# Splitting the first weight chunk into two column halves, and the last values product into two halves of 128 columns

## The chip, the core and the metric

The kernel runs on one core of a Trainium2 chip. The time is the device time of one execution in microseconds (us); for the kernel before it is the median of three runs. The profile is of one further execution. TensorE (PE) multiplies, VectorE (DVE), ScalarE (ACT) and GpSimd (POOL) do the rest, and SyncE (SP) issues most transfers. In a profile "PEld" is TensorE's loading of a stationary operand, and "SPq", "ACTq" and "POOLq" are what the engines' sequencers issue.

## What is computed

For x of shape 2 x 2048 x 512 in float32 (cut from the reference):

```python
xn = _layernorm(x, axis=-1)
# attention on xn: a second layer norm with gamma and beta, one head of width 512, causal
q, k, v = x_norm @ qkv[:, :KEY], x_norm @ qkv[:, KEY:2 * KEY], x_norm @ qkv[:, 2 * KEY:]
s = softmax(causal(q @ k.T / sqrt(KEY))) @ v @ o_proj + residual
# mixture of experts on xn: 8 experts, the best 2 of each token, silu between two layers
g = _silu(_L0_ffn_ref(xn, ...))
x = x + s * g
```

## The kernel before, in words

The 4096 rows are 32 tiles of 128 rows, in 8 blocks of four tiles. A first stage multiplies weights with one another, so that later only two products of the normalized rows are needed: `wqk` is the product of the query and key weights (`fold`, L221), `wvo` that of the value weights and `o_proj` (`fold_by_seven`, L247). It also normalizes the rows block by block, makes queries and values from them and stores them to DRAM. A second stage routes the tokens and computes the experts. A third computes attention and the output, tile by tile, in pairs. Everything is float32, and from L867 on each engine gets its instructions in the order of the Python text (`manual_schedule`).

**The opening.** Six small matmuls on zeros (`warm`, L872) run while nothing has arrived. `load_raw(c, pair)` (L214) issues chunk `c` (128 rows of 512 columns) of two weights, the first of the pair on SP's queue and the second on ScalarE's. For chunk 0 of the first weight there are two transfers already, columns 0 to 127 and 128 to 511. After chunk 1, `load(0)` (L169) brings the rows of block 0, tiles 0 and 2 on SP's queue, 1 and 3 on ScalarE's. Then come chunks 2 and 3 of the pair, and four chunks of the second pair. Ten transfers stand in ScalarE's queue ahead of its first computation, the square root of the first block's variances in `rstd_of` (L130), with the load of its function table.

In the built program each transfer of the two hardware queues, SP's and ScalarE's together, takes the next of eight completion semaphores. The issue of a transfer waits until the one that had this semaphore before, eight places earlier, has landed. The numbering goes through both queues about alternately.

`fold` multiplies chunk by chunk: for each of the four chunks there are four matmuls, one for each block `r` of 128 rows of the result, into four accumulators `banks`. A float32 matmul of the text is two instructions in the profile, each with its own weight load. The first matmul takes the first 128 columns of chunk 0 of one weight as stationary operand and all 512 columns of chunk 0 of the other as moving operand.

Meanwhile VectorE takes statistics of the rows (`norm_stats`, L304), waits for ScalarE's root, and makes z (`norm_rows`, L326); GpSimd splits z into halves (`zu`, L347), SP turns these by transposing transfers (`zuT`, L354) and stores them (`zu_d`, L357). VectorE also makes the sums that `fold_by_seven` needs (L239, L245). Of each block ScalarE makes the keys `kT` (L379) and issues their store to `kt_d` (L384) from its own queue, among its copies of TensorE's results (L549, L552, L555, L569).

**The end.** The last two tiles, `AHEAD` (L1709), are finished by `values_end(s)` (L1618) with s = 30. The values of the pair come from seven products instead of eight, in halves of 256 columns, `LO` and `HI`. Accumulators are `p57`, `p64` and `p03`, from a pool of three banks that are taken in turn (`bank`, L1589). The last product is the lower half of the second tile: `chain` (L1576) over six blocks of the combined weights, and `product` (L1527) over the four blocks left over, both into `p64[:, HI]`. Before it stand in VectorE's order the preparations that don't need it: `u3` is multiplied by the gate and added to the gate's tile. Then `emit_ahead` (L1727) takes the product from its accumulator, multiplies it by the row's divisor and the gate (`gated`, L1723), adds the prepared part (L1596) and issues the store on SP's queue (L1731):

```python
def emit_ahead(s, o, cols, attention=None):
    xt, _ = gates[s]
    gated(o[:, cols], o[:, cols] if attention is None else attention, s, cols)
    add(o[:, cols], o[:, cols], xt[:, cols])
    nc.sync.dma_start(out=ob[:, seq[s], cols], in_=o[:, cols])
```

Of the kernel before, what the change touches and what calls it, by code (L numbers as in the profile page):

```python
# [20 lines left out]
P = 128  # L21
# [5 lines left out]
def gated_attention_moe(  # L27
# [28 lines left out]
    nc = tc.nc  # L56
    B, S, D = x.shape
# [8 lines left out]
    NK = KEY // P  # L66
# [147 lines left out]
    def load_raw(c, pair):  # L214
        for i, queue in zip(pair, (nc.sync, nc.scalar)):

            cuts = (0, P, D) if c == 0 and i == 0 else (0, D)
            for at in (slice(*cut) for cut in zip(cuts, cuts[1:])):
                queue.dma_start(out=parts[i][:, c, at], in_=srcs[i][ts(c, P), at])

    def fold(dst, lhs, rhs, scale):  # L221
        pws = banks
        for c in range(NK):
            for r in range(ND):
                nc.tensor.matmul(
                    pws[r], lhsT=lhs[:, c, ts(r, P)], rhs=rhs[:, c, :],
                    start=(c == 0), stop=(c == NK - 1),
                )
        for r in range(ND):
            nc.scalar.mul(dst[:, r, :], pws[r], scale)  # L230

# [641 lines left out]
    for c in range(NK):  # L873
        load_raw(c, (0, 1))
        if c == 1:
            load(0)
    for c in range(NK):
        load_raw(c, (2, 3))
    load_small()
    load(1)  # L880
    fill_rows()
    norm(0)
    fold(wqk, parts[0], parts[1], 1.0 / math.sqrt(KEY))
    fold_sums = four(4), four(5)
    for k in ((0,), (1,), (2, 3)):
# [384 lines left out]
    def place(s):  # L1270
        b, t = divmod(seq[s], BT)
        return b, t, b - b % NBB
# [142 lines left out]
    for i in range(NM):  # L1415
# [21 lines left out]
        for _ in range(3):  # L1437
            if i >= paired.stop and early:
                f, b, c = early.pop(0)
# [83 lines left out]
    def place_keys(s):  # L1523

        return place(s)[1] + 1 + (place(s)[0] - place(s)[2]) * BT

    def product(dst, s, k0, k1, cols, start=True):  # L1527

        first = place(s)[2]
        for k in range(k0, k1):  # L1530
            nc.tensor.matmul(  # L1531
                dst, lhsT=turned[s][:, ts(k, P)], rhs=avs[first + k // BT][:, k % BT, cols],
                start=(start and k == k0), stop=(k == k1 - 1),
            )
# [5 lines left out]
    LO, HI = slice(0, D // 2), slice(D // 2, D)  # L1540
# [35 lines left out]
    def chain(dst, a, v, stop=True):  # L1576
        n = a.shape[1]
        for k in range(n):
            nc.tensor.matmul(  # L1579
                dst, lhsT=a[:, k], rhs=v(k), start=(k == 0), stop=(stop and k == n - 1)  # L1580
            )

    def vt(s, i):
        return lambda k: avts[place(s)[2] + k // 2][:, k % 2, i, :]

    def raw(s, half, cols):
        return lambda k: avs[place(s)[2] + k // 2][:, 2 * (k % 2) + half, cols]

    def bank(s, name):  # L1589
        return ps_b.tile([P, D], F32, name=f"{name}_{s}", tag="b")  # L1590

    def half_d(s, name):
        return cp.tile([P, D // 2], F32, name=f"{name}_{s}", tag=name)

    def add(out, a, b):
        nc.vector.tensor_tensor(out, a, b, ALU.add)  # L1596
# [21 lines left out]
    def values_end(s, meanwhile=()):  # L1618
        m, _, _, a22, _, s2, _, s4 = combos.pop(s)
        p1, o1, p57 = seven.pop(s)  # L1620
        u2, u3 = half_d(s, "u2"), half_d(s, "u3")
        o2 = op.tile([P, D], F32, name=f"o_{s + 1}", tag="o", bufs=4)
        k1, k2 = place_keys(s), place_keys(s + 1)
        p64, p03 = bank(s, "p64"), bank(s, "p03")
        chain(p64[:, LO], s2, vt(s, 1))
        add(u2, p64[:, LO], p1)
        add(u3, p57[:, HI], u2)
        add(o2[:, HI], p57[:, LO], u3)
        add(u2, p57[:, LO], u2)
        product(p03[:, LO], s + 1, 2 * m, k2, HI)  # L1630
        chain(p03[:, HI], s4, raw(s, 1, HI), stop=False)
        product(p03[:, HI], s, 2 * m, k1, HI, start=False)
        add(o1[:, HI], p03[:, HI], u2)
        if s in AHEAD:
            emit_ahead(s, o1, HI)
        add(o2[:, HI], p03[:, LO], o2[:, HI])
        if s in AHEAD:
            emit_ahead(s + 1, o2, HI)
        for f in meanwhile:
            f()  # L1640
        if s in AHEAD:

            gated(u3, u3, s + 1, LO)
            add(gates[s + 1][0][:, LO], u3, gates[s + 1][0][:, LO])
        chain(p64[:, HI], a22, vt(s, 3), stop=False)
        product(p64[:, HI], s + 1, 2 * m, k2, LO, start=False)
        if s in AHEAD:
            emit_ahead(s + 1, o2, LO, p64[:, HI])
        else:
            add(o2[:, LO], p64[:, HI], u3)  # L1650
        outs[s], outs[s + 1] = o1, o2

# [68 lines left out]
    def gated(out, a, s, cols):  # L1721

        nc.vector.scalar_tensor_tensor(  # L1723
            out, a, sums[s], gates[s][1][:, cols], ALU.mult, ALU.mult
# [7 lines that stand above are left out]
# [24 lines left out]
    for s in range(NT + OUT + 2):  # L1756
# [92 lines left out]
        elif s == 3:  # L1849
# [8 lines left out]
            for f, *args in joins:  # L1858
                f(*args)
            values_end(0, [lambda: query_sums(s + 1, nc.vector)])  # L1860
        elif s == NT:
            emit_ahead(s - 2, seven[s - 2][1], LO)
            values_next(s - 2)
        elif fast and s % 2 == 0:
            values_first(s - 2)

            if s != NT - 2:
                values_next(s - 2)
        elif fast and s == NT - 1:
            values_next(s - 3)  # L1870
            values_end(
                s - 3,
                [lambda: join_p(s)] * len(halves[s])
                + [lambda: combine_p(s - 1, (1, 3)), lambda: gate(s - 1)]
                + [lambda: combine_p(s - 1, (2, 4))],
            )
        elif fast:
            values_end(s - 3)
        elif 0 <= s - 2 < NT and not (s - 1 < NT and by_te(s - 1)):
            values(s - 2)  # L1880
# [56 lines left out]
```

## Time and profile before

| | us |
|---|---|
| median of three runs (lowest, highest) | 1010.59 (1010.33, 1010.79) |
| the profiled execution: its time, its span | 1012.02, 1010.3 |
| TensorE's first instruction | 1.13 |
| VectorE's first statistics | 8.40 |
| first 256-column pass of the last product | 1001.98 |
| transfer of the last store, issue to landing | 1.7 |
| VectorE, ScalarE, GpSimd: idle within the span | 29%, 60%, 52% |

The span goes from the first to the last instruction on the core, and the execution's own time has some 1.7 us more. The page gives the granted TensorE clock as full over the whole span. The core's transfers are busy to 80% and more in the first seven slices of 25 us, at 230 to 330 GB/s.

Views used below are the page itself, the timeline (instructions of an engine in order of time, like ones merged: start, duration, engine, line, operation, output<-input, shapes, count, and in brackets the idle time before it with what ended it), the list of waits, the groups by line and shape, and the transfers of a window. A wait is put down to the releaser that came last by the profile.

### The profile page before, as it was taken

To read this page: it belongs to the slowest core of one execution; us is meant where nothing else is said; L and a number is where in the kernel's file an instruction comes from. 1 tells how busy PE (TensorE), PEld (TensorE's weight loads), DVE (VectorE), ACT (ScalarE), POOL (GpSimd) and SP (SyncE) were. 2 spreads that over 40 slices of the span, in tenths; PEclk is the share of its full clock that TensorE was granted. 3 is DMA by queue.
4 is the path that set the end of the run, shared out by engine and by line. 5 is a ranking of instruction groups with operands and counts; after the bars stand their busy time and mean duration, and the time that the engine had idled before them with its cause. 6 is when DMAs were issued, how large, how long until landed. Compare 5 with 4: busy or idle time off the path is not lost. (4 is left out here: it accounts for less than half of the span.)

```text
span 1010.3 us, 13408 instructions
## 1 busy us (share of the span) xinstructions
PE 1001.5 (99%) x3924; PEld 665.7 (66%) x3924; DVE 719.6 (71%) x1396; ACT 402.7 (40%) x804; POOL 481.6 (48%) x475
## 2 busy tenths in 40 slices
PE   9999999999999999999999999999999999999998
PEld 5887888874577677667653448677675544447577
DVE  6997755896877777776744669678576457878667
ACT  3354455322444544444455122232345544442241
POOL 4474465003744444443432256164557776764272
PEclk9999999999999999999999999999999999999999
DMA  8799987979999999999999576373677768753361
GB/s 291 234 240 319 319 237 268 331 254 230 182 247 213 205 219 218 210 211 214 213 213 254 162 191 149 90 189 110 186 199 233 224 202 241 204 146 86 95 164 42
DMA packets 295495, 207.96 MB, mean 206 GB/s; under 512 B 230648, under 2 KB 243704, under 8 KB 294400
## 3 DMA queue, kind: packets, MB, share of 16 engines
q1 hardware_dynamic: 280128, 155.17, 62.1%
q0 software_dynamic: 10400, 34.63, 12.6%
q10 hardware_dynamic: 4896, 17.30, 4.6%
q8 instruction: 34, 0.56, 0.2%
q14 instruction: 37, 0.30, 0.1%
HBM read 92.35 MB, written 60.03 MB: 151 GB/s over the span
## 5 line engine op out<-in xcount | busy, mean ns | idle before, releaser
L1191 PE MATMUL py<-arena,ht 128*128 (+3 forms) x396 | 176.7, 593 | 0.0
L1303 PE MATMUL ps<-k,q 128*128 128x512 f32 (+3 forms) x416 | 143.0, 495 | 0.3 <-PEq L1451 0.3
L1491 POOL COPY pu<-pT 128x1024 uint16<-128x1024 uint16 (+2 forms) x74 | 81.8, 1137 | 119.1 <-ACT pT L1481 59.2
L1162 POOL COPY hu<-h 128x704 uint16<-128x704 uint16 x66 | 61.8, 954 | 155.8 <-issue 121.7
L1191 PEld LDWEIGHTS py<-arena,ht 128*128 128x128 f32 (+3 forms) x396 | 71.8, 185 | 80.6 <-issue 76.4
L1303 PEld LDWEIGHTS ps<-k,q 128*128 128x128 f32 x416 | 74.7, 190 | 67.1 <-issue 56.3
L966 POOL DMA_INDIRECT xs<-zu_d,toki x66 | 77.7, 1177 | 70.6 <-DVE toki L793 55.9
L1177 ACT ACTIVATE ht<-ht,b1sel 128x128 f32<-128x128 f32 (+3 forms) x216 | 67.9, 380 | 88.4 <-DVE ht L1171 88.4
L1141 DVE TENSOR_TENSOR h<-p,h 128x176 f32<-128x176 f32 x182 | 55.4, 336 | 59.6 <-PE p L1134 56.1
L1674 POOL DMA_INDIRECT yg<-y_d,posi x64 | 67.3, 1052 | 36.9 <-DVE yg L1685 22.0
L1531 PE MATMUL po<-v,pT 128*128 128x512 f32 x152 | 67.9, 592 | 0.0
L347 POOL COPY zu<-z 128x1024 uint16<-128x1024 uint16 x32 | 39.4, 1230 | 57.7 <-DVE z L332 57.7
L1481 ACT ACTIVATE pT<-pT,nm 128x1024 f32<-128x1024 f32 x14 | 16.1, 1148 | 110.3 <-DVE nm L1391 72.0
L1513 DVE COPY pT<-puT 128x1024 uint16<-128x1024 uint16 (+2 forms) x74 | 53.4, 750 | 7.4 <-DMA puT<-pu 7.2
L1199 ACT COPY y<-py 128x512 f32<-128x512 f32 x55 | 32.1, 584 | 62.1 <-PE py L1191 48.2
L1481 ACT ACTIVATE pT<-ps,nm 128x512 f32<-128x512 f32 (+3 forms) x52 | 30.0, 580 | 60.4 <-DVE nm L1391 36.7
L1361 DVE TENSOR_TENSOR pT<-p,pT 128x512 f32<-128x512 f32 x49 | 32.9, 687 | 25.8 <-PE p L1355 22.1
L1531 PEld LDWEIGHTS po<-v,pT 128*128 128x128 f32 x152 | 28.6, 190 | 31.9 <-issue 30.1
L1042 DVE COPY xT<-xhT 128x1024 uint16<-128x1024 uint16 x66 | 44.7, 703 | 6.4 <-DMA xhT<-xs 6.3
L1703 POOL TENSOR_TENSOR o<-o,yg 128x512 f32<-128x512 f32 x30 | 41.4, 1380 | 14.3 <-DVE o L1695 14.2
L1695 DVE SCALAR_TENSOR_TENSOR o<-xo,xscale,o 128x512 f32<-128x512 f32 x30 | 25.9, 871 | 30.1 <-ACT o L1692 30.1
L1704 POOL TENSOR_TENSOR o<-o,xo 128x512 f32<-128x512 f32 x30 | 43.2, 1439 | 2.4
(342 smaller groups left out, 2146.9 us busy)
## 6 DMA issues: line engine op xcount, KB each, us to landing
y_d<-y SPq DMA_DIRECT2D x66, 256.0 KB, 4.3
zu_d<-zu SPq DMA_DIRECT2D x32, 264.0 KB, 3.2
kt_d<-kT ACTq DMA_DIRECT2D x8, 1024.0 KB, 8.2
q<-qt_d SPq DMA_DIRECT2D x32, 256.0 KB, 5.0
k<-kt_d SPq DMA_DIRECT2D x32, 256.0 KB, 4.2
v<-v_d SPq DMA_DIRECT2D x32, 256.0 KB, 5.7
xo<-in_x_dram SPq DMA_DIRECT2D x32, 256.0 KB, 4.0
x<-in_x_dram SPq DMA_DIRECT2D x30, 256.0 KB, 6.5
```

The costliest lines, as they stand in the source:

```text
L966: nc.gpsimd.indirect_dma_start(out=xs, out_offset=None, in_=zu_d, in_offset=bass.IndirectOffsetOnAxis(ap=toki[:, order[i] : order[i] + 1], ...
L1042: nc.vector.tensor_copy(xT.bitcast(U16).rearrange("p c (t h) -> p c t h", h=2), xhs.pop(i).rearrange("p (h c) t -> p c t h", h=2),)
L1141: nc.vector.tensor_tensor(out, x, y, ALU.add)
L1162: nc.gpsimd.tensor_copy(hu[:, :, :H], h.bitcast(U16).rearrange("p (d h) -> p h d", h=2))
L1177: nc.scalar.activation(ht[:hn, c, at], ht[:hn, c, at], AF.Silu, bias=b1sel[:hn, c, j : j + 1])
L1191: nc.tensor.matmul(py[at, :], lhsT=ht[:k, c, at], rhs=rhs[n], start=(c == 0), stop=(c == NH - 1),)
L1303: nc.tensor.matmul(ps[:, :w], lhsT=aqs[seq[s] // 2][:, c, ts(t % 2, P)], rhs=aks[first + j][:, c, :w], start=(c == 0), stop=(c == ND - 1),)
L1481: nc.scalar.activation(turned[s][:, at:end], src, AF.Exp, bias=nm, accum_out=rs[:, j : j + 1])
L1491: nc.gpsimd.tensor_copy(pu[:, : 2 * w].rearrange("p (h d) -> p h d", h=2), turned[s][:, k : k + w].bitcast(U16).rearrange("p (d h) -> p h ...
L1513: nc.vector.tensor_copy(turned[s][:, k : k + w].bitcast(U16).rearrange("p (i t h) -> p i t h", t=P, h=2), puT[:, : 2 * w // P, :].rearrang ...
L1531: nc.tensor.matmul(dst, lhsT=turned[s][:, ts(k, P)], rhs=avs[first + k // BT][:, k % BT, cols], start=(start and k == k0), stop=(k == k1 - 1),
L1674: nc.gpsimd.indirect_dma_start(out=y, out_offset=None, in_=y_d, in_offset=bass.IndirectOffsetOnAxis(ap=posi[k][:, n : n + 1], axis=0),)
```

## The change

Chunk 0 of the second weight of the first pair, which was one transfer of 512 columns on ScalarE's queue, becomes two of 256 columns there. The first matmul of `fold` becomes two, one for each half of the columns, into the halves of the same accumulator; only the first of them starts the accumulation.

In `values_end`, for the last pair only, the last product is made in two halves of 128 columns one after the other, the first into its old place in `p64`, the second into the same columns of a further bank `p6` from the same pool. Each half is finished and stored by its own `emit_ahead`. All other pairs keep the old form.

```diff
     def load_raw(c, pair):
         for i, queue in zip(pair, (nc.sync, nc.scalar)):
 
-            cuts = (0, P, D) if c == 0 and i == 0 else (0, D)
+            cuts = (0, D) if c else {0: (0, P, D), 1: (0, D // 2, D)}.get(i, (0, D))
             for at in (slice(*cut) for cut in zip(cuts, cuts[1:])):
                 queue.dma_start(out=parts[i][:, c, at], in_=srcs[i][ts(c, P), at])
...
         for c in range(NK):
             for r in range(ND):
-                nc.tensor.matmul(
-                    pws[r], lhsT=lhs[:, c, ts(r, P)], rhs=rhs[:, c, :],
-                    start=(c == 0), stop=(c == NK - 1),
-                )
+                for h in (slice(0, D // 2), slice(D // 2, D)) if r + c == 0 else (slice(0, D),):
+                    nc.tensor.matmul(
+                        pws[r][:, h], lhsT=lhs[:, c, ts(r, P)], rhs=rhs[:, c, h],
+                        start=(c == 0 and h.start == 0), stop=(c == NK - 1), skip_group_check=True,
+                    )
...
-        chain(p64[:, HI], a22, vt(s, 3), stop=False)
-        product(p64[:, HI], s + 1, 2 * m, k2, LO, start=False)
         if s in AHEAD:
-            emit_ahead(s + 1, o2, LO, p64[:, HI])
+            for cols in (slice(0, P), slice(P, 2 * P)):
+                dst = (bank(s, "p6") if cols.start else p64)[:, HI][:, cols]
+                chain(dst, a22, lambda k: vt(s, 3)(k)[:, cols], stop=False)
+                product(dst, s + 1, 2 * m, k2, cols, start=False)
+                emit_ahead(s + 1, o2, cols, dst)
         else:
+            chain(p64[:, HI], a22, vt(s, 3), stop=False)
+            product(p64[:, HI], s + 1, 2 * m, k2, LO, start=False)
             add(o2[:, LO], p64[:, HI], u3)
```

## The prediction

> **What bounds the kernel now.** I read the engine shares first, then TensorE's waits, then the first 14 us and the last 10 us instruction by instruction.
>
> ```profile
> PE 1001.5 (99%) x3924; PEld 665.7 (66%) x3924; DVE 719.6 (71%) x1396; ACT 402.7 (40%) x804; POOL 481.6 (48%) x475
> ...
> PE bank_a L526 <- ACT raw L552: 1.4, 1, 1.4
> PE warm L872 <- DVE b1s L181: 1.1, 1, 1.1
> PE bank_b L526 <- ACT bank_c L555: 0.7, 1, 0.7
> ```
>
> TensorE is busy 1001.5 of 1010.3 us, so a change of its first and last microseconds can only move the 9 us that are left, unless it moves a wait inside. Those waits (each line: who waited for whom, total us, times, longest) are few. The longest, 1.4 us, decides what a gain at the start is worth.
>
> The opening (start, duration in us, then engine and what it did):
>
> ```profile
> 0.81 0.90 ACTq L219 DMA_DIRECT2D raw<-in_qkv_t_dram  x2
> 1.13 2.93 PE L872 MATMUL warm<-gw 128*128 128x128 f32 x12 [1.13 <-DVE b1s L181]
> 4.06 0.50 PEld L225 LDWEIGHTS bank_a<-raw 128*128 128x128 f32 x2 [0.30 <-DMA raw<-in_qkv_t_dram]
> 5.92 1.19 PE L225 MATMUL bank_b<-raw 128*128 128x512 f32 x2
> 7.50 4.06 ACTq L219 DMA_DIRECT2D raw<-in_o_proj_dram  x4
> 11.59 1.28 ACT L130 ACT_TABLE_LOAD   x1 [11.59 <-DMA raw<-in_qkv_t_dram]
> 12.88 0.21 ACT L130 ACTIVATE sd_a<-va 128x8 f32<-128x8 f32 x1
> 13.13 0.20 DVE L132 RECIPROCAL r_a<-sd_a 128x8 f32<-128x8 f32 x1 [0.94 <-ACT sd_a L130]
> ```
>
> Two things are to be seen. The first real weight load comes 0.30 us after the last one of the warming passes; it waits for data. And ScalarE's first computation waits until its own queue has issued ten transfers: the last issue ends at 11.56, the table load follows, then the root, and VectorE has stood 0.94 us for it. From 13.13 to 66 us the waits of VectorE show none on TensorE, and on ScalarE only its next root (0.27 us): its chain (fold sums, statistics, roots, rows for GpSimd, transposes) runs at its own pace from that root on.
>
> Where that chain meets TensorE:
>
> ```profile
> 81.49 0.33 ACTq L384 DMA_DIRECT2D kt_d<-kT  x1
> 82.34 0.59 ACT L552 COPY raw<-bank_a 128x512 f32<-128x512 f32 x1
> 82.99 1.99 PE L526 MATMUL bank_a<-kT,wqk 128*128 128x256 f32 x8 [1.40 <-ACT raw L552]
> ```
>
> ScalarE stands idle for 4.55 us before L569, because the store of block 2's keys ahead of it in its queue is not issued before 81.49. In the built program a transfer's issue waits for the one eight places earlier; here that is a store of `zu` of block 3 on SP, whose rows GpSimd had finished at 73.1 from z of VectorE's 65.6. So TensorE's 1.40 us come from VectorE's chain, not from its own past: what TensorE gains before 82.99 it waits there.
>
> **What the Trainium skill says.** "DMA: Bandwidth & Descriptors", section Queues, rings and completion order: each DMA engine goes round-robin between the queues, packet by packet. The trace agrees; from 3.0 to 3.2 us the two queues (ScalarE's q10, SP's q1; packets, MB, share) moved as many packets each, of unlike size:
>
> ```profile
> q10 hardware_dynamic: 29, 0.05, 64.4%
> q1 hardware_dynamic: 30, 0.03, 40.8%
> ```
>
> "TensorE: Matmul & The Clock Gate", What's actually happening: the array runs at half rate until it was busy for a window of about 3.4 us. Here passes of 512 columns start 0.85 apart (5.07, 5.92) and 0.43 apart from 6.5 on; so time won before the switch is worth half, unless the switch comes earlier too. The same page, section "Wait — 56ns, not 53.3ns?", gives a fixed cost of about 2.5 ns per matmul; halving columns therefore costs something, and the trace has the price itself (below).
>
> **Part 1, the first chunk.** The transfers are numbered about alternately on the two queues. By their issue waits, ScalarE's first (256 KB, chunk 0 of the keys' weights) landed at about 4.03, where SP's fifth issue starts, and SP's first (64 KB) by 3.78, where ScalarE's fifth starts. So the 256 KB are the gate, as halving them supposes. Eight packets per engine of SP's first and ScalarE's first are 4 + 16 = 20 KB; with the half they are 4 + 8 = 12 KB. 16 engines x 8 KB = 128 KB at the 0.39 MB/us of that stretch: 0.33 us sooner, 3.7. The warming passes start 0.227 apart, the last at 3.63, so the weight load can go at about 3.75 instead of 4.06: 0.3 us. The second half lands by the 16th packet, 32 KB, about 4.4, and is wanted 0.85 later than the first, at 4.7; SP's remaining 192 KB landed at 4.85, wanted at about 5.1 as before. Four passes of 256 take the place of two of 512 (0.2155 us apart against 0.43: nothing). Worth: 0.15 (switch of the clock stays) to 0.3 us.
>
> What is queued behind the added issue: ScalarE's eleven instead of ten transfers. Its queue gets packets one for one with SP's, so every later transfer of it lands eight packets per engine later. Before, its transfers land beside SP's in rounds of eight packets: at 20 KB per engine 4.0, at 48 KB 5.0, at 80 KB 7.3 (SP's third, by the issue at 7.1; ScalarE's third, 7.5), at 112 KB 8.5, at 144 KB 9.6 to 10.2, at 176 KB 11.1 to 11.2. The last is ScalarE's chunk 3, for which its last issue waits. After, chunk 3 is the seventh instead of the sixth transfer there, and lands with SP's seventh at 12 + 20 + 5 x 32 = 192 KB. SP's seventh landed at 12.0 with 208 KB, so 192 KB lie at 11.6. The last issue, table load, root and so VectorE's chain: 0.4 us later (bounds: 0, if the order of the numbers lets the issue wait on SP's earlier transfer or if va, ready at 12.19, were the gate; 0.65, a whole 256 KB). Nothing hides it: the next op of VectorE is the one that had waited 0.94. The inputs of the statistics land earlier or as before, so they hide nothing either. TensorE itself wants this chain's z at 18.5 (done 16.8, then 17.2) and s, t at 22.8 (18.4, then 18.8): covered. At 82.99 it isn't: TensorE restarts 0.4 us later and its early start is swallowed; I expect 1.4 + 0.4 + 0.2 = 2.0 us of wait there. Part 1: +0.4.
>
> **Part 2, the last product.**
>
> ```profile
> 777.68 1.06 PE L1303 MATMUL ps<-k,q 128*128 128x128 f32 x8
> ...
> 1001.98 2.75 PE L1579 MATMUL p<-vT,pT 128*128 128x256 f32 x12
> 1004.57 1.89 PE L1531 MATMUL p<-v,pT 128*128 128x256 f32 x8
> 1006.50 0.48 DVE L1723 SCALAR_TENSOR_TENSOR o<-p,ri,yg 128x256 f32<-128x256 f32 x1 [0.74 <-PE p L1531]
> 1007.02 0.42 DVE L1596 TENSOR_TENSOR o<-o,xo 128x256 f32<-128x256 f32 x1
> 1007.47 0.33 SPq L1731 DMA_DIRECT2D out_dram<-o  x1
> ```
>
> Now: 20 passes of 256 columns, (2.75 - 0.379)/11 = 0.2155 us apart, end 1006.46; then VectorE, SP, landing 1.7 us after the issue. After: 40 passes of 128. The row of 128 columns with own weight loads gives (1.06 - 0.275)/7 = 0.111 apart, so 39 x 0.111 + 0.275 = 4.60 from 1001.98: end 1006.58, +0.12 (bounds 0 and +0.25). The first half is done at 1001.98 + 19 x 0.111 + 0.275 = 1004.36; VectorE is at L1723 and L1596 for u3 until 1005.75, then does this half by 1006.45 and SP issues it by 1006.8: hidden. The second half: L1723 and L1596 lose 128 of 256 columns. L1308 (128x128) takes 0.292, L1596 at 256 columns 0.424, so 0.13 each, 0.27 in all. Store at 1006.58 + 0.04 + 0.39 + 0.29 + 0.03 = 1007.33 against 1007.47. Its packets: 1 KB ones took 46 ns each (1008.2 to 1008.8), 512-byte ones 28 ns (1.8 to 2.0); eight per engine: 0.37 against 0.23, -0.14 (0 to -0.2). Part 2: -0.14 - 0.14 = -0.28 (bounds -0.05 and -0.4). The second half's bank is the third request after the one of `p57`, whose last reader ended at 1000.44: no wait.
>
> **Sum.** +0.4 - 0.28 = +0.1 us. The profiled execution took 1012.02 for its span of 1010.3; the median of three runs is 1010.59, spread 0.46. I add the change to the median: 1010.7. What this kernel can tell from no change is about 0.2%, 2.0 us; both parts lie far below.
>
> **Rivals.**
> - VectorE's chain doesn't move: the last issue of ScalarE comes at 11.2 as before. For it: the two queues' numbers could be dealt so that the wait falls on SP's earlier chunk; against it: one transfer more in a queue that gets packets one for one. 1010.59 - 0.28 = 1010.3.
> - The start counts: the chain comes earlier, or the wait at 82.99 isn't its. For it: inputs land earlier; against it: root behind ScalarE's issues. 1010.59 - 0.28 - 0.3 = 1010.0.
> - Slower: the new bank isn't free. If the three banks turn so that the second half meets a tile whose reader is still to come (the first half's own), TensorE stops after 1004.36 until VectorE has read at 1006.12, and 4.60/2 us follow: store at about 1009.1, -0.14, so +1.5, with part 1 +1.9: 1012.5. It decides as soon as the second half's first pass starts after 1004.5. Against it: the count above.
>
> **Numbers.** Chain later (my forecast) 0.52, own range 1010.4 to 1011.1; chain unmoved 0.27; start counts 0.13; bank 0.04; something of the opening's shift growing on its way to 83 us (VectorE's ops there take 0.68 or 1.5 us beside GpSimd) 0.04. The range 1009.9 to 1011.3 leaves out the last two and a little of the third. Faster by over 0.2% would need 2 us from 9 us of idle: 0.03. Slower: half the bank's chance and of the last case: 0.04. Same: 0.93.
>
> **What would show it.** First weight load near 3.75; ACT table load near 12.0 and root near 13.3; wait for L552 near 2.0 us and bank_a starting near 83.4; last pass ending 1006.6 and last store issued 0.75 us after it, both moved by the shift. If the table load stays at 11.6, the second case holds; if bank_a starts before 82.9, the third. A sum over 2 us either way would mean a wait that I haven't seen.

## The result, and the profile after

| | median, us | runs (lowest, highest) | ratio to before, 95% interval |
|---|---|---|---|
| before | 1011.08 | 20 (1010.33, 1013.08) | |
| after | 1012.39 | 20 (1011.41, 1017.59) | 1.0014 [1.0008, 1.0021] |

The change costs 1.3 us, or 0.14%. The forecast was 1010.7, the range 1009.9 to 1011.3: the time lies above it. I had held about 0.2% to be the least that this kernel can tell from no change; with 20 runs of each, the interval of 0.14% lies clear of one. Of the 1.7 us between forecast and time 0.5 belong to the base, whose median over 20 runs is 1011.08 where three runs had given 1010.59. On that base the range would have ended at 1011.8, which is still too low.

The profiled execution after took 1012.14 us, span 1010.4. That of before took 1012.02, but it lay 0.9 above its median. So I profiled the kernel before a second time: 1010.95 us, span 1009.2. That execution, called the second profile below, is at the median; the one that the prediction used is the first.

The opening of the kernel after (timeline: start, duration, engine and instruction):

```profile
3.64 0.55 PEld L226 LDWEIGHTS bank_a<-raw 128*128 128x128 f32 x2
3.85 1.78 PE L226 MATMUL bank_a<-raw 128*128 128x256 f32 x4
...
8.15 0.30 PEld L226 LDWEIGHTS bank_a<-raw 128*128 128x128 f32 x2 [0.78 <-DMA raw<-in_qkv_t_dram]
...
11.99 0.30 PEld L226 LDWEIGHTS bank_a<-raw 128*128 128x128 f32 x2 [0.96 <-DMA raw<-in_qkv_t_dram]
...
13.67 1.28 ACT L130 ACT_TABLE_LOAD   x1 [13.67 <-DMA raw<-in_o_proj_dram]
14.97 0.21 ACT L130 ACTIVATE sd_a<-va 128x8 f32<-128x8 f32 x1
...
15.21 0.20 DVE L132 RECIPROCAL r_a<-sd_a 128x8 f32<-128x8 f32 x1 [2.35 <-ACT sd_a L130]
```

The start is 0.42 us earlier than before's 4.06, as meant. Then the transfers of chunks 1 and 2 come late, which the brackets of the third and fourth line show; and ScalarE's table load starts at 13.67 where it started at 11.59 (11.39 in the second profile). VectorE stands 2.35 us for the root instead of 0.94 (1.28 in the second profile).

The same 2 us can be followed to TensorE. First SP's transposing transfers and stores of block 3 in the kernel after, then the same lines of the kernel before in its second profile:

```profile
69.00 7.26 SPq L355 DMA_TRANSPOSE zuT<-zu  x4
76.31 2.98 SPq L358 DMA_DIRECT2D zu_d<-zu  x4
```

```profile
67.03 7.25 SPq L354 DMA_TRANSPOSE zuT<-zu  x4
74.33 3.41 SPq L357 DMA_DIRECT2D zu_d<-zu  x4
```

Then ScalarE and TensorE in the kernel after, at the place that the prediction had named, and TensorE there in the second profile of before:

```profile
81.99 0.33 ACTq L385 DMA_DIRECT2D kt_d<-kT  x1
82.36 0.58 ACT L570 COPY raw<-bank_c 128x512 f32<-128x512 f32 x1 [4.04 <-PE bank_b L527]
82.84 0.59 ACT L553 COPY raw<-bank_a 128x512 f32<-128x512 f32 x1
...
83.48 1.78 PE L527 MATMUL bank_a<-kT,wqk 128*128 128x256 f32 x7 [0.89 <-ACT raw L553]
```

```profile
81.92 1.99 PE L526 MATMUL bank_a<-kT,wqk 128*128 128x256 f32 x8 [0.84 <-ACT raw L552]
```

Put side by side (start of each step, us):

| step | before, first | before, second | after |
|---|---|---|---|
| table load | 11.59 | 11.39 | 13.67 |
| first reciprocal of VectorE | 13.13 | 12.93 | 15.21 |
| z of block 3 | 65.59 | 65.11 | 67.08 |
| block 3's transposing transfers (how long) | 67.51 (8.37) | 67.03 (7.25) | 69.00 (7.26) |
| block 3's stores of zu | 75.94 | 74.33 | 76.31 |
| store of block 2's keys | 81.49 | 80.42 | 81.99 |
| bank_a multiplied again | 82.99 | 81.92 | 83.48 |
| time of that execution | 1012.02 | 1010.95 | 1012.14 |
| time less the line above it | 929.03 | 929.03 | 928.66 |

Two things are to be seen. From the second profile to after the delay is 2.28 us at the root, 1.98 at the stores of zu, 1.56 where TensorE restarts. And what follows that restart takes the same time in every kernel of this document but one (no_cut, below): 928.9 to 929.1 us, with the new tail 928.7. So the moment at which TensorE gets on near 83 us sets the result. The first profile's extra 1.07 us arose on this chain as well: 0.20 at the root, 0.28 on VectorE up to the transposing transfers, 1.12 in those transfers themselves, and about 0.5 given back between the start of the stores of zu and the store of the keys.

TensorE's waits (total, times, longest) show the place as well, with one that is new, the third line:

```profile
PE bank_a L527 <- ACT raw L553: 0.9, 1, 0.9
PE bank_b L527 <- ACT bank_c L556: 0.7, 1, 0.7
PE bank_c L527 <- ACT raw L540: 0.7, 1, 0.7
```

The new wait lies at 49.7 us. Here are ScalarE and TensorE in the kernel after, then ScalarE in the second profile of before:

```profile
47.81 0.21 ACT L130 ACTIVATE sd_a<-va 128x8 f32<-128x8 f32 x1 [5.42 <-DVE va L319]
49.00 0.59 ACT L540 COPY raw<-bank_c 128x512 f32<-128x512 f32 x1
...
49.74 1.97 PE L527 MATMUL bank_c<-arena,wqk 128*128 128x256 f32 x8 [0.67 <-ACT raw L540]
```

```profile
45.84 0.21 ACT L130 ACTIVATE sd_a<-va 128x8 f32<-128x8 f32 x1 [4.05 <-DVE va L318]
47.03 0.59 ACT L539 COPY raw<-bank_c 128x512 f32<-128x512 f32 x1
```

ScalarE takes another block's root there as soon as VectorE's variances are ready, and that is 2.0 us later than in the second profile; its copies stand behind the root, and TensorE needs the last of them. So VectorE's late chain meets TensorE here already, before it does so near 83 us.

Why chunk 3 lands so late is in the transfers of the opening, from 3.5 to 6.5 us, first in the second profile of before and then after:

```profile
DMA packets 673, 1.19 MB, mean 396 GB/s; under 512 B 71, under 2 KB 162, under 8 KB 673
```

```profile
DMA packets 465, 0.78 MB, mean 259 GB/s; under 512 B 49, under 2 KB 130, under 8 KB 465
```

The issues agree: SP's seventh, which waits for a landing, comes at 7.94 after and at 6.29 in that profile.

The end of the kernel after:

```profile
1002.49 1.50 PE L1580 MATMUL p<-vT,pT 128*128 128x128 f32 x12
...
1006.06 1.06 PE L1532 MATMUL p<-v,pT 128*128 128x128 f32 x8
1006.18 0.34 DVE L1728 SCALAR_TENSOR_TENSOR o<-p,ri,yg 128x128 f32<-128x128 f32 x1
1006.56 0.29 DVE L1597 TENSOR_TENSOR o<-o,xo 128x128 f32<-128x128 f32 x1
1007.15 0.35 DVE L1728 SCALAR_TENSOR_TENSOR o<-p,ri,yg 128x128 f32<-128x128 f32 x1 [0.30 <-PE p L1532]
1007.54 0.29 DVE L1597 TENSOR_TENSOR o<-o,xo 128x128 f32<-128x128 f32 x1
...
1007.86 0.33 SPq L1736 DMA_DIRECT2D out_dram<-o  x1
```

The forty passes take 4.63 us (in the first profile of before the twenty took 4.48), the first half is finished on VectorE while the second is multiplied, and the last store is issued 0.74 us after the last pass.

### The profile page after: what moved, and what is told of

Same layout as the page of the kernel before. It is cut to its first block, busy times and chain, and to the rows that moved or that the text cites. A ratio compares the mean times of both kernels' runs of the same rounds, so it can differ in the third digit from the quotient of the medians.

```text
span 1010.4 us, 13457 instructions
## 1 busy us (share of the span) xinstructions
PE 1001.9 (99%) x3946; PEld 667.4 (66%) x3946; DVE 719.1 (71%) x1398; ACT 402.7 (40%) x804; POOL 480.9 (48%) x475
```

## The experiments

The letters in the expectations: A, the late root, carried by VectorE's chain, makes the loss; B, the tail makes it; C, TensorE's own waits in the opening make it. P, the same rows of the two weights side by side slow the transfers; N, the number of transfers does; S, rows of 1 KB do. All results first; the rate is the mean of 3.5 to 6.5 us, and the three columns after it come from one profiled execution.

| kernel | GB/s | table load | bank_a | its time | ratio of the runs, 95% interval |
|---|---|---|---|---|---|
| before_again (unchanged) | 396 | 11.39 | 81.92 | 1010.95 | 0.9997 [0.9986, 1.0008] |
| after_again (the change) | 262 | 13.67 | 83.48 | 1012.17 | 1.0009 [1.0001, 1.0018] |
| front_only | 309 | 13.38 | 83.21 | 1012.18 | 1.0013 [1.0006, 1.0019] |
| tail_only | 402 | 11.34 | 82.97 | 1011.70 | 0.9993 [0.9987, 1.0000] |
| load_halves | 272 | 13.61 | 83.51 | 1012.48 | 1.0015 [1.0006, 1.0025] |
| matmul_halves | 391 | 11.27 | 82.15 | 1011.18 | 1.0002 [0.9991, 1.0013] |
| no_cut | 389 | 12.15 | 81.86 | 1011.53 | 1.0014 [1.0005, 1.0023] |
| three_cuts | 242 | 12.86 | 83.22 | 1012.15 | 1.0003 [0.9995, 1.0012] |
| front_root | 277 | 10.97 | 82.02 | 1010.99 | 0.9998 [0.9989, 1.0007] |
| tail_root | 382 | 9.46 | 82.17 | 1010.91 | 1.0002 [0.9991, 1.0014] |
| row_halves | 297 | 13.14 | 85.54 | 1014.51 | 1.0026 [1.0016, 1.0036] |
| sp_halves | 361 | 11.50 | 82.32 | 1011.38 | 1.0002 [0.9994, 1.0010] |
| act_only | 391 | 12.45 | 83.96 | 1012.98 | 1.0014 [1.0007, 1.0021] |
| sp_three | 390 | 11.66 | 81.77 | 1010.75 | 0.9999 [0.9990, 1.0007] |
| later_cut | 397 | 11.77 | 82.30 | 1011.30 | 0.9999 [0.9991, 1.0008] |
| after_root | 234 | 11.16 | 82.65 | 1011.31 | 1.0000 [0.9991, 1.0008] |

Executions of one kernel lie 1 us and more apart, so a single profile is read for its order of events, and the ratio for the time.

**The two parts alone, and both kernels again.** front_only has the cut load and the cut first matmul, tail_only the two halves of the last product.

> Part 1 alone (first chunk in two halves). Theory A, ScalarE's queue of eleven transfers delays its root and with it VectorE's chain: +1.5 us (ratio 1.0015), table load near 13, root near 14.5 us, and a wait of TensorE near 83 us that ends later than before's. Rival B, the loss lies in the tail: ratio 1.000. Rival C, TensorE loses in the opening itself by its waits for chunks 1 and 2: the transposes of z start later than before's 18.97 by the whole loss.

> Part 2 alone (last product in two halves). Theory A: -0.2 to -0.3 us (ratio 0.9998), the last pass ends 4.6 us after the first of the product instead of 4.48, and the last store is issued 0.75 us after it. Rival B: +1.3 us or more, with a gap between the two halves on TensorE or a later landing of the last store.

> The kernel before, unchanged, for a second profile and the spread of its times. Every theory: ratio 1.000 within 0.0005. If the profile on record was typical, TensorE waits 1.4 us for ScalarE near 83 us again; if it was one of the slower executions (its 1012.0 us lie 0.9 above the median of 20 runs), the wait is shorter, near 0.5 us, and bank_a restarts near 82.

> The changed kernel again, for a second profile. Theory A: ratio 1.0012, the sum of the two parts alone; table load near 13.7 us as in its first profile, if the delay is the program's and not that execution's.

Part 1 costs 0.13%, and part 2 gains some 0.07%, with an interval that just reaches no change. The sum lies within the interval of after_again, though below the 0.14% of the first comparison. B falls: the time behind bank_a is 928.7 with the new tail and 929.0 without it, so the tail gains 0.3 us.

**Part 1 in two.** load_halves cuts only the transfer (first line), matmul_halves only the first matmul (second line).

```diff
+            cuts = (0, D) if c else {0: (0, P, D), 1: (0, D // 2, D)}.get(i, (0, D))
...
+                for h in (slice(0, D // 2), slice(D // 2, D)) if r + c == 0 else (slice(0, D),):
```

> Only the transfer of part 1 in two halves; the first matmul stays whole, the last product too. If the loss comes from the transfers: ratio 1.0013 as for part 1 alone, table load near 13.4, 240 to 300 GB/s from 3.5 to 6.5 us. If it comes from the split matmul: 1.000, table load near 11.4.

> Only the first matmul of part 1 in two halves, from one transfer of 256 KB. Transfers theory: ratio 1.000, table load near 11.4, first weight load near 4.05, 350 to 420 GB/s from 3.5 to 6.5 us. Rival: the loss stays (1.0013).

The cut transfer alone brings the whole loss. Four passes of 256 columns in place of two of 512 cost nothing that shows: the interval of matmul_halves is wide, but its table load, its restart of bank_a and its transfers are those of the kernel before.

**Which rows run side by side.** no_cut takes SP's old cut away, so that both weights' chunk 0 are whole; three_cuts is part 1 with SP's chunk 0 in three pieces, so that the two queues are out of step.

```diff
-            cuts = (0, P, D) if c == 0 and i == 0 else (0, D)
+            cuts = (0, D)
```

```diff
+            cuts = (0, D) if c else {0: (0, P, 5 * P // 2, D), 1: (0, D // 2, D)}.get(i, (0, D))
```

> The kernel before without the cut of SP's first transfer: one transfer less, and both queues bring the same chunk of the two weights side by side, as with part 1. Theory P, the same rows of the two weights side by side slow the transfers: under 300 GB/s for some 2.5 us of the first 7, ScalarE's table load later than 11.6 although its queue holds only ten transfers, ratio 1.0005 or more. Theory N, it is the number of transfers in ScalarE's queue (or the small ones): 350 to 420 GB/s from 3 us on, table load at 11.4 or earlier, ratio 1.000 with a first weight load 0.2 to 0.5 us later.

> Part 1 with one more cut of SP's first chunk (columns 0, 128, 320, 512): eleven transfers on ScalarE's queue as with part 1, but the two queues are again one transfer apart as before. Theory P: 350 to 420 GB/s from 3.5 to 6.5 us, table load near 12 (0.4 to 0.7 us later than before for the eleventh transfer), ratio 1.0003 or so. Theory N: table load near 13.4 as with part 1, ratio 1.0013.

P falls: side by side and whole the transfers ran at 389 GB/s, out of step and cut at 242. The times of these two kernels I can't explain in full. no_cut's ratio is 1.0014 though its profiled execution restarts bank_a at 81.86, and it is the one kernel whose time behind bank_a is not near 929.0 or 928.7 but 929.67; in that execution 0.6 us are lost between 251 and 260 us, at the start of the experts, where VectorE's longest wait for a transfer is 5.4 us, and 2.2 in the second profile of before. three_cuts has the low rate and a late table load, 12.86, yet a ratio of 1.0003; its interval reaches to 1.0012, and its profiled execution, 0.6 above its median, has slow transposing transfers (7.78 us against 7.25).

**The root ahead of the transfers.** The direct test of A: front_root is part 1, with the same cut and the same transfers, but ScalarE takes the first root before its last two issues. tail_root is part 2 with the root before the last issue (3 in place of 2 in the edit).

```diff
     for c in range(NK):
+        if c == 2:
+            norm_stats(0)
+            norm_roots(0)
         load_raw(c, (2, 3))
...
-    norm(0)
+    norm_rows(0)
```

> Part 1 alone, and ScalarE takes the first root before its last two transfers instead of after all eleven. Same transfers, same rows, same matmuls as in part 1 alone. Theory A (the loss of part 1 is the late root, carried by VectorE's chain to TensorE's wait near 83 us): table load near 11.3 instead of 13.4, root near 12.8 (then va is what it waits for), issue of block 2's key store near 80.4 to 81.0, bank_a again near 81.9 to 82.5, ratio 0.999 to 1.001 against 1.0013 of part 1 alone. Theory C (TensorE's own waits for chunks 1 and 2 in the opening): the ratio stays at 1.0013, bank_a near 83.

> Part 2 alone, and ScalarE takes the first root before its last transfer. Theory A: in the kernel before the root waits for that transfer too; here it comes with va at about 11.8 to 12.2 instead of 12.7 to 12.9, TensorE's wait near 83 us (0.8 to 1.4) shrinks by as much, and the time falls by 0.5 to 0.9 us on top of part 2's 0.3: ratio 0.9985 to 0.9992. Theory C: 0.9995, as part 2 alone.

The timeline of front_root:

```profile
10.97 1.28 ACT L130 ACT_TABLE_LOAD   x1 [10.97 <-DMA raw<-in_qkv_t_dram]
12.53 0.21 ACT L130 ACTIVATE sd_a<-va 128x8 f32<-128x8 f32 x1 [0.27 <-DVE va L319]
12.77 0.20 DVE L132 RECIPROCAL r_a<-sd_a 128x8 f32<-128x8 f32 x1 [0.28 <-ACT sd_a L130]
...
82.02 1.99 PE L527 MATMUL bank_a<-kT,wqk 128*128 128x256 f32 x8 [0.71 <-ACT raw L553]
```

The transfers are as slow as in the change (277 GB/s from 3.5 to 6.5 us), and the loss is gone: the root now waits for its input va, bank_a is multiplied again at 82.02 and the ratio is 0.9998 against 1.0013. TensorE's weight loads still wait for chunks 1 and 2 (0.49 and 0.94 us, in front_only 0.58 and 0.85), so these waits don't make the loss. A holds for the change, and C falls. The edit moves a second thing: ScalarE's last two transfers are issued only from 14.09 on, and VectorE waits 0.79 us for one of them; the gain comes in spite of that.

tail_root was to gain as much again, and doesn't: its first root comes 0.8 us earlier than in tail_only, but VectorE gives that back in block 1. GpSimd and VectorE of tail_root, then of tail_only:

```profile
26.84 1.27 POOL L486 TENSOR_TENSOR arena<-kT,arena 128x512 f32<-128x512 f32 x1 [1.53 <-ACT kT L379]
26.90 1.24 DVE L317 TENSOR_SCALAR va<-mv 128x4 f32<-128x4 f32 x1
28.48 0.20 DVE L132 RECIPROCAL r_a<-sd_a 128x8 f32<-128x8 f32 x1 [0.27 <-ACT sd_a L130]
29.30 1.27 POOL L488 TENSOR_TENSOR arena<-kT,arena 128x512 f32<-128x512 f32 x1
29.39 1.19 DVE L135 TENSOR_TENSOR c_a<-c_a,va 128x8 f32<-128x8 f32 x1
```

```profile
26.76 1.27 POOL L486 TENSOR_TENSOR arena<-kT,arena 128x512 f32<-128x512 f32 x1 [1.32 <-ACT kT L379]
27.55 0.51 DVE L317 TENSOR_SCALAR va<-mv 128x4 f32<-128x4 f32 x1
28.40 0.20 DVE L132 RECIPROCAL r_a<-sd_a 128x8 f32<-128x8 f32 x1 [0.27 <-ACT sd_a L130]
29.31 1.19 DVE L135 TENSOR_TENSOR c_a<-c_a,va 128x8 f32<-128x8 f32 x1
```

At L317 tail_root is still 0.65 us ahead. The operation takes 1.24 us instead of 0.51 and ends, as it does in tail_only, with GpSimd's operation (28.1); the lead is gone. Both kernels then lose time at L135, which takes 1.19 us and ends with GpSimd's operation of L488 (30.6 in tail_root). In the second profile of before, L135 starts at 29.65, after GpSimd's last one has ended, and takes 0.17: its z of block 1 starts at 30.36, those of tail_root and tail_only at 31.13 and 31.05. The Trainium skill, "GPSIMD Engine Reference", section 1. Specifications, says that GpSimd's interfaces to SBUF, the on-chip memory, are shared with VectorE and collide with VectorE's instructions of two SBUF inputs, among others. L135 has two such inputs, c_a and va, and its lines agree; L317 has only mv, and no run here shows why it waits.

**What of the cut makes the transfers slow.** row_halves cuts ScalarE's chunk 0 by partitions, in two of 64 with rows of 2 KB; sp_halves moves SP's old cut to column 256; act_only cuts ScalarE's chunk and leaves SP's whole; sp_three cuts SP's in three and leaves ScalarE's whole; later_cut leaves both as before and cuts ScalarE's first x tile. The edit of row_halves, and then those of the other four in this order:

```diff
+            if (c, i) == (0, 1):
+                for h in (0, HALF):
+                    queue.dma_start(out=parts[i][h : h + HALF, c, :], in_=srcs[i][h : h + HALF, :])
+                continue
```

```diff
+            cuts = (0, D // 2, D) if c == 0 and i == 0 else (0, D)
...
+            cuts = (0, D // 2, D) if c == 0 and i == 1 else (0, D)
...
+            cuts = (0, P, 5 * P // 2, D) if c == 0 and i == 0 else (0, D)
...
+            for at in (slice(0, D // 2), slice(D // 2, D)) if b == 0 and t == 1 else (slice(0, D),):
+                queue.dma_start(out=xt[:, t, at], in_=xb[:, b * BT + t, at])
```

> ScalarE's chunk 0 cut by partitions (64 and 64) instead of by columns: eleven transfers in its queue as in the change, but rows of 2 KB, so as many packets as before. The matmul is whole. Theory N (the number of transfers): rate from 4 to 6.5 us below 310 GB/s, table load near 13.5, ratio 1.0013. Theory S (the rows of 1 KB, so more packets): rate above 350 GB/s in those windows, table load 11.3 to 11.9, ratio 0.9995 to 1.0003.

> The kernel before with SP's chunk 0 cut at column 256 instead of 128 (two transfers with rows of 1 KB); ScalarE's chunk 0 whole, ten transfers. Theory S in the form that rows of 1 KB are slow by themselves: rate from 4 to 6.5 us below 310 GB/s, table load above 12.5. In the form that only both queues' short rows together, or the alignment of the two queues, lower it: above 350 GB/s, table load 11.3 to 11.7, first weight load a little later than 4.06 (about 4.2), ratio 0.9995 to 1.0003.

> ScalarE's chunk 0 in column halves, SP's chunk 0 whole (matmul whole): ScalarE's queue holds eleven transfers, SP's one fewer, 21 in the opening as before. If eleven in ScalarE's queue are the cause: rate from 3.5 to 6.5 us below 310 GB/s, table load above 13. If the number of both queues together, or both queues' chunk 0 cut, is the cause: above 350 GB/s, table load 11.3 to 12.0. First weight load later than in the kernel before in both cases (SP's 256 KB are its gate), 4.3 or later.

> SP's chunk 0 in three (columns 0, 128, 320, 512), ScalarE's whole: 22 transfers in the opening, ten of them ScalarE's. If the number of both queues together is the cause: rate below 310 GB/s, table load 12.5 or later. If eleven in ScalarE's queue, or both chunk 0 cut, is the cause: above 350 GB/s, table load 11.3 to 11.9, ratio 0.9995 to 1.0005.

> The kernel before with ScalarE's first x tile loaded in two column halves: 22 transfers, eleven of them ScalarE's, both loads of chunk 0 as before. If either number is the cause: rate below 310 GB/s, table load 13 or later, ratio 1.001. If both chunk 0 cut is the cause: above 350 GB/s, table load 11.6 to 12.2, ratio 0.9995 to 1.0005.

The transfers of act_only from 3.5 to 6.5 us, in the form shown above:

```profile
DMA packets 718, 1.17 MB, mean 391 GB/s; under 512 B 77, under 2 KB 215, under 8 KB 718
```

With the same two transfers of 1 KB rows in ScalarE's queue, eleven in all, the rate stays high; so does it with 22 transfers in the opening (sp_three), with 22 of which eleven are ScalarE's (later_cut), and with SP's rows of 1 KB (sp_halves). It falls in every kernel in which the first weight chunk of both queues is cut, however it is cut. N and S as single causes fall. Why both cuts together do it stays open. row_halves gives no clean answer on the length of rows: its rate falls most in one half microsecond (107 GB/s from 3.5 to 4.0, 369 and more from 5.5), ScalarE's first three issues took 0.56 to 0.61 us instead of 0.41 to 0.46, and TensorE waited 1.68 us for the second half of its chunk.

What the number of transfers costs by itself can be read from two of these kernels. With eleven transfers in ScalarE's queue at the full rate the table load is at 11.77 (later_cut) and 12.45 (act_only), against 11.27 to 11.66 in those with ten and SP's cut. act_only's time has a second cause: its first real matmul waits for SP's whole 256 KB:

```profile
5.33 1.19 PE L225 MATMUL bank_a<-raw 128*128 128x512 f32 x1 [1.27 <-DMA raw<-in_qkv_t_dram]
```

The keys and GpSimd's sums come later with it: the sum of L486 starts at 28.57 (25.86 in the second profile of before), after 1.54 us of waiting for the keys, and VectorE's operations beside it last until it ends, as in tail_root. At bank_a TensorE then waits only 0.17 us, and in row_halves 0.33. From the first reciprocal to z of block 3 it is 53.6 us in act_only and 54.3 in row_halves, against 51.9 after the change. By this reading of two profiles a late first matmul (5.3 and 5.7 us) adds a loss of its own; in the change it isn't late.

**The whole change with the root ahead.** after_root is the change with the edit of front_root.

> The whole change, with the first root ahead of ScalarE's last two transfers. Theory A: bank_a again near 82.0, time near 82.0 + 928.7 = 1010.7, ratio 0.9992 to 1.0000 against 1.0014 of the whole change: part 2's 0.3 us are left, part 1 gives nothing. If part 1's earlier start counted once the root is free: 1010.3 or less, ratio below 0.9990.

The loss is gone, and nothing is gained that shows: ratio 1.0000, bank_a at 82.65. With the root free, part 1's earlier start has no visible worth, and not even part 2's 0.3 us stand out of the spread. Of the versions that I ran, tail_only alone has an interval that doesn't reach beyond 1.0000.

## Why the prediction was wrong

- **What bounds the kernel: right.** The chain from ScalarE's root over VectorE, GpSimd and SP's transfers to the store of block 2's keys sets TensorE's restart near 83 us, and TensorE's own early start is swallowed there: front_only loses although its weight load came earlier, and front_root, which only puts the root ahead of two issues, gets all of it back.
- **The start: right.** The weight load came at 3.64 (3.75 expected), and the second half of the chunk had landed by 4.6 (4.4).
- **The step that failed** is a term of part 1's sum: "chunk 3 ... lands with SP's seventh at 12 + 20 + 5 x 32 = 192 KB. SP's seventh landed at 12.0 with 208 KB, so 192 KB lie at 11.6", hence 0.4 us, bounds 0 and 0.65. The count of the kilobytes ahead fits the kernels at the full rate, where the eleventh transfer puts the table load at 11.77 and 12.45 (12.0 expected). But I dated them by the rate of the kernel before, and both cuts together bring the rate down to 234 to 309 GB/s from 3.5 to 6.5 us. The table load came at 13.67: 2.1 later than in the first profile, 2.3 than in the second, of which 1.2 lie beyond act_only's 12.45. The upper bound took the amount of data as unsure and the rate as given. Part 1 so cost 1.3 us (front_only) instead of 0.4. The same step made the inputs of the statistics land "earlier or as before"; the first statistics came at 9.30 instead of 8.40, which the still later root hid.
- **From the root to 83 us: right in kind, smaller in size.** I let the delay arrive whole. Of 2.28 us 1.56 arrived. VectorE's stretches beside GpSimd took up 0.3 of the rest (the operation of L317 in the kernel before took 0.49 us instead of 0.80, in block 1), the steps from the stores of zu to that of the keys 0.4.
- **The wait for L552: wrong, 0.89 instead of 2.0.** The sum added the delay to the first profile's 1.40 and counted 0.2 for TensorE's lead. TensorE had lost that lead before. Its weight loads waited 0.78 and 0.96 for chunks 1 and 2, which the sum doesn't have because it took their transfers to keep their pace; its passes came later by less, and at 14.67 TensorE was level with the first profile. At 49.7 it waited 0.67 more. I had named 82.99 as the first place where VectorE's chain isn't covered, and it meets TensorE at 49.7 already, over ScalarE's root.
- **The start of the sum.** bank_a came at 83.48, 0.1 from the 83.4 that I wrote. That is no merit: my 83.4 was 0.4 after a first profile that was itself 1.07 late. The expected time was added to the median, to which bank_a near 81.9 belongs.
- **The tail: right.** Passes 4.63 us (4.60 expected, where the quotient 0.785 / 7 is 0.112 and not 0.111, which gives 4.65), last store 0.74 us after the last pass (0.75). From bank_a to the end it is 0.29 to 0.37 us shorter (0.28 expected, bounds 0.05 and 0.4); most of it after the store's issue: 4.28 us from there to the end of the execution, against 4.55.
- **The rivals.** The chain did move, the start didn't count, and the bank was free: the passes of both halves follow each other without a gap. Nearest was the last case, a shift of the opening that grows, to which I gave 0.04; but it grew in the opening itself, among the transfers.

## What to carry to other kernels

Here an engine that issues transfers and then starts a long chain paid for one transfer more in its queue; look for the first computation that stands behind issues, and put it ahead of those it doesn't need. When a load is cut, take the rate as unknown too, and let the bound of the cost reach as far as the slowest stretch of the trace. And take a second execution of the kernel before as a base: here two of them differ by 1.07 us at the very wait that decides, which is nearly as much as the change costs.

## What the runs showed of the hardware

- Cutting the first chunk on one of the two queues or on neither left the transfers at 361 to 402 GB/s (3.5 to 6.5 us; 342 in the first profile of before); cutting both brought 234 to 309, and after the change the low rate lasts some 2 us beyond the last short row of the two chunks, which starts at 4.1. The single packets in the trace show where it goes: of those with 2 KB that started from 3 to 6.5 us, 88% took the usual 75 to 95 ns after the change too, but 13 of 335 took 400 or more, in the second profile of before 1 of 573. The longest took 1.06 to 2.0 us in the kernels with both cuts and 0.15 to 0.75 in the others. What holds these few up stays open.
- The Trainium skill, "DMA: Bandwidth & Descriptors", Specifications, has 512 B as the least size for the full rate; sp_three, whose shortest rows have just 512 B, agrees with 390 GB/s, and the kernels with both cuts, whose rows have 512 B and more, show that this size doesn't secure it.
- Some small VectorE operations end only with GpSimd's 1.27 us operation if they start beside it: on eight columns 0.17 becomes 1.19 (L135), on four it was up to 1.24 (L317). The statistics don't: in the second profile of before one of them runs at 25.89 beside GpSimd's operation of 25.86 and takes its usual 0.66. A lead of 0.65 us was lost in this way in tail_root. The way from the first reciprocal to the restart of bank_a took 68.2 to 70.1 us (row_halves apart); TensorE's late start in act_only and the transposing transfers have a share in that.
- Four transposing transfers took 7.23 to 8.37 us for the same rows. The longest falls in the first profile of the kernel before.
